# Powers on GpSimd in place of square roots and their corrections, in an eigensolver that runs under a graph network's products

## The chip, the cores and the metric

One core of a Trainium2 chip runs the program. The time is that of the device, in microseconds, as the median of three executions; a separate profiled execution gives the trace. Everything is computed in fp32. The engines are named as in the profile: PE (TensorE), with PEld for its weight loads, DVE (VectorE), ACT (ScalarE), POOL (GpSimd) and SP (the queue that issues the DMAs).

## What is computed

Two residual layers on `x` of 64 batches, 256 nodes and 256 features, with an adjacency matrix of 256 x 256. Layer 0 is three graph convolutions with the element-wise square of the adjacency; layer 1 needs the eigenvectors of a normalized Laplacian and applies a small network between `U.T` and `U`.

```python
def _L0_gnn_ref(x, adj, S, W1, W2, W3):          # S is adj
    def _slconv(x, adj, S, W):
        support = jnp.einsum('bnf,fh->bnh', x, W)
        return jnp.einsum('nm,bmh->bnh', adj * S, support)
    h = jax.nn.relu(_slconv(x, adj, S, W1))      # 256 -> 512
    h = jax.nn.relu(_slconv(h, adj, S, W2))      # 512 -> 1024
    return _slconv(h, adj, S, W3)                # 1024 -> 256

def _L1_gnn_ref(features, A, W1, b1, W2, b2):
    deg = jnp.sum(A, axis=0) + jnp.sum(A, axis=1) - jnp.diagonal(A)
    d_inv_sqrt = jnp.where(deg > 0, jax.lax.rsqrt(deg), 0.0)
    L_norm = d_inv_sqrt[:, None] * (jnp.diag(deg) - A) * d_inv_sqrt[None, :]
    _, U = jnp.linalg.eigh(L_norm)
    h = jax.nn.relu(jnp.einsum('mn,bnd->bmd', U.T, features) @ W1 + b1)
    return jnp.einsum('nm,bmd->bnd', U, h @ W2 + b2)

h = jnp.maximum(_layernorm(x, axis=-1), 0.0)
x = x + _L0_gnn_ref(h, adj, adj, W1, W2, W3)
h = jnp.maximum(_layernorm(x, axis=-1), 0.0)
x = x + _L1_gnn_ref(h, adj, W1, b1, W2, b2)
```

## The kernel before

**Two kinds of work share the core.** The eigensolver (class `Eigen`) is a long chain of small dependent instructions, mostly on DVE, with a few products on PE and a few copies and square roots on ACT. Layer 0 (class `Layers`) is a large amount of dense products on PE, whose results ACT copies or rectifies out of PSUM. Layer 1 can begin only when the eigenvectors are there. The 64 batches are worked on as 32 pairs; layer 0's results of most pairs are written to DRAM and fetched again for layer 1.

**The planner sets the order on PE and ACT.** Every instruction passes as an `Op` (line 83) through a `Pace` (line 161). `Op` gives each a planned duration by engine and size; for POOL it is `0.2 + 2 * n / 960` us for n elements in a partition. `Pace` keeps a planned clock for each engine. `chain` (line 211) takes an instruction of the eigensolver: it works out when its operands would be ready, and `run` (line 227) first issues as many instructions of the two layer-0 streams as fit ahead of that moment, cutting a product's columns in two where that fits better. `issue` (line 209 calls the instruction) multiplies the planned durations of the chain by `slower`: 1.06 as a rule (`SLOWER`), 1.13 in the leaves (`IN_BLOCKS`). The order made so is final for PE and ACT, which work through their queues in order. On DVE, POOL and SP the tile framework orders the instructions itself by its own estimates. Since nearly all instructions pass through `issue`, most rows of the profile carry L209; those after the planner is switched off carry L213.

**The stages of the chain**, in order:

- `laplacian` (line 402): degrees, their inverse square root `dinv` (by `root`, line 349: a square root on ACT, then a reciprocal, two sums or products and a scaling on DVE, then one more reciprocal), the matrix `A`.
- `tridiagonalize` (line 439): 254 Householder steps, `k` from 0. While `lo = k + 1` is under 128, a step works on both halves of the rows (the wide half), then on the second alone (the narrow half). `below` takes the sum of squares below the diagonal (`tail`), `length` the squared length `nn`, its root `s0` on ACT, half the sign `q` and `qn = q * nn`; the step then takes `rs = 1 / s0`, `qs = q * s0`, and `nb = rs * qn + qs`. In the trace nb is written to `m`. In the wide half `q`, `qn`, `qs`, `gg`, `gu` and part of `xc` run on POOL (`aside`), in the narrow half on DVE. `none` and a copy of `alpha` run on POOL in both. Two groups of transposes on PE bring the columns `ac` (as `psB<-ident,ac`) and `A`'s column (as `psA<-ident,A`) into rows; four long updates write the two halves of `A` at the end of a step, of which some stand behind the next step's `nn` on DVE.
- `reflections` (line 583), a third stream, forms the product of the reflections during the first part of `leaves` (line 983), which solves the 16 x 16 blocks on DVE with small roots on ACT and one copy on POOL in each iteration.
- `level` (line 1304), four times, for blocks of 32, 64, 128 and 256: it merges pairs of blocks. Its products are, in order, `psC<-ident,dnew`, `psC<-m,dnew`, `psA<-A,m`, `psA<-q,m`, `psB<-ident,m` and `psA<-q,m`. Between the first `psA<-q,m` and `psB<-ident,m` lies `rational_steps` (line 1213): a start and five iterations, each with one root of a [128, 2] column `dq` (in the trace `rdq`) on ACT. Then come `zh` and `rn`, each a `root` and a reciprocal. Ahead of the first `psA<-q,m` stands a root of a 256-wide row (`sq`).
- `vectors` (line 1718) ends the chain with a flag (`psC<-bad`), and the program branches on it; the branch that would solve again is not taken.

**The norms of layer 0.** `norm` (line 1835) serves both layer norms, once for each pair: ACT sums the four rows of a pair into `s`, DVE makes the negated mean `nm`, ACT sums the squares into `v`, DVE scales `v`, ACT takes the root, and five DVE instructions correct it and form `scale` and `shift`, which ACT needs for the normalized ReLU `h`.

**The end.** `layer1` (line 2131) runs layer 1's 32 pairs in a pipeline of three stages. What is left of layer 0 is put between its products; ahead of its ninth round, `pace.finish()` issues all that is still left. The pairs 30 and 31 stay on chip and come as the twelfth and thirteenth.

Of the kernel before, what the change touches and what calls it, by code (L numbers as in the profile page):

```python
# [82 lines left out]
class Op:  # L83
# [4 lines left out]
    def __init__(self, part, call, args, kwargs):  # L88
# [14 lines left out]
        if self.engine == "PE":  # L103
            self.columns = 0 if "transpose" in self.name else n
            self.busy = max(n * self.COLUMN, 0.224) if self.columns else 0.115
            self.until = max(self.busy, 0.165) + 0.35
        elif self.engine == "ACT":
            pointers = any(isinstance(kwargs.get(k), bass.AP) for k in ("scale", "bias"))
            self.busy = 0.13 + n / 1400 + 0.12 * pointers + 0.19 * sums
            self.until = self.busy + 0.12  # L110
        elif self.engine == "DVE":
            each = 6.3 if self.name == "reciprocal" else 2.0 if self.name == "tensor_tensor_scan" else 1.0
            pointers = self.name == "scalar_tensor_tensor" or any(a.shape[1:] == [1] for a in ins[1:])
            self.busy = 0.065 + 0.06 * pointers + each * n / 960 + 0.08 * sums
            self.until = self.busy + 0.125
        elif self.engine == "POOL":
            self.busy = 0.2 + 2 * n / 960
            self.until = self.busy + 0.1
        else:
            self.busy, self.until = 0.1, 4.0  # L120
# [40 lines left out]
class Pace:  # L161
# [5 lines left out]
    WINDOW = 1.0  # L167
    SLOWER, IN_BLOCKS = 1.06, 1.13
    LATER = {"PE": 0.4, "ACT": 0.1}
# [111 lines left out]
class Eigen:  # L281


    def __init__(self, tc, ctx, ap, gt2, pace):
# [11 lines left out]
        self.iota, self.far, self.ones = (pool.tile([P, N], F32, name=c) for c in ("iota", "far", "ones"))  # L296
        tc.nc.vector.memset(self.ones, 1.0)

        self.nc.scalar.activation(self.far[:, 0:1], self.ones[:, 0:1], AF.Sqrt)
# [46 lines left out]
    def recip(self, out, a):  # L346
        return self.nc.vector.reciprocal(out, a)

    def root(self, out, a, tmp, scale=1.0):
# [52 lines left out]
    def laplacian(self):  # L402
# [13 lines left out]

        safe, rt, tmp = self.col("c3"), self.col("c4"), self.col("c5")
        self.ts(safe, deg, 1e-30, OP.max)
        self.root(rt, safe, tmp)
        dinv = self.col("c6")  # L420
        self.recip(dinv, rt)
        self.stt(dinv, deg, 0.0, dinv, OP.is_gt, OP.mult)
# [16 lines left out]
    def tridiagonalize(self, a):  # L439
# [43 lines left out]
        def length(xr, lo, tail):  # L483

            nn, s0, q, qn = (self.col(c, 1) for c in ("nn", "s0", "q", "qn"))
            x1 = xr[:, lo : lo + 1]
            self.stt(nn, x1, x1, tail, OP.mult, OP.add)
            nc.scalar.activation(s0, nn, AF.Sqrt, bias=guard)
            aside(lo).tensor_scalar(q, x1, 0.0, 0.5, OP.is_ge, OP.subtract)
            aside(lo).tensor_tensor(qn, q, nn, OP.mult)  # L490
            return nn, s0, q, qn
# [7 lines left out]
        for k in range(N - 2):  # L499
# [5 lines left out]

            rs, qs, nb = self.col("rs", 1), self.col("qs", 1), nbs[:, k : k + 1]
# [24 lines left out]
            gc, gr = self.col("gc"), row("gr")  # L531
            self.ts(gc[:, hs], ac[:, hs], gam, OP.mult)

# [679 lines left out]
    def rational_steps(self, n, kd, zsum, zown, znxt, acc, s, gap, half, y, bs, rb):  # L1213
# [33 lines left out]
        for step in range(ROOT_STEPS):  # L1247
# [40 lines left out]
            self.ts(dq, dq, 1e-36, OP.max)  # L1288
            nc.scalar.activation(dq, dq, AF.Sqrt)
            self.tt(b, b, dq, OP.add)  # L1290
# [13 lines left out]
    def level(self, n, qt, dc, rho, sg, bad=None):  # L1304
# [452 lines left out]
class Layers:  # L1757


    def __init__(self, tc, ctx, ap, gt2, u, ut):  # L1760
# [22 lines left out]
        self.u1 = pool.tile([P, H], F32, name="u1")  # L1783
        self.ub2 = pool.tile([P, H, N], F32, name="ub2")

    def load_weights(self):
# [48 lines left out]
    def norm(self, x, scale, shift, parts=range(4)):  # L1835
# [3 lines left out]
        at = slice(parts[0], parts[-1] + 1, parts[1] - parts[0])  # L1839
        s, nm, v, tmp = (self.sp.tile([P, g], F32, tag=c, name=c) for c in ("s", "nm", "v", "tmp"))  # L1840
        for j in parts:
            junk = self.sp.tile([P, N], F32, tag="junk", name="junk", bufs=1)
            yield nc.scalar.activation(junk, x[:, j // 2, j % 2, :], AF.Copy, accum_out=s[:, j : j + 1])
        yield nc.vector.tensor_scalar(nm[:, at], s[:, at], -1.0 / N, None, OP.mult)
        for j in parts:
            junk = self.sp.tile([P, N], F32, tag="junk", name="junk", bufs=1)
            yield nc.scalar.activation(
                junk, x[:, j // 2, j % 2, :], AF.Square, bias=nm[:, j : j + 1], accum_out=v[:, j : j + 1]
            )
        s, nm, v, tmp, scale, shift = (t[:, at] for t in (s, nm, v, tmp, scale, shift))  # L1850
# [371 lines left out]
```

## Time and profile before

| | |
|---|---|
| median of 3 executions | 2425.47 us (2423.66 to 2426.67) |
| the profiled execution's own time | 2425.03 us |
| its span, first to last instruction | 2423.2 us |
| PE busy | 2380.5 us, 98% of the span, 9222 records |
| DVE busy | 2074.8 us, 86%, 12688 |
| ACT busy | 1014.1 us, 42%, 2827 |
| POOL busy | 479.1 us, 20%, 1752 |
| DMA | 90 MB, 37 GB/s on average; 250 GB/s from 2300 us on |
| chain of waits that ended last | PE from 2183 us to the end, but for 5.2 us at 2279 to 2285 |

Busy time is what an engine's records cover; a matmul's end is modelled, so that a PE that is busy all the time may still have small pauses between the starts of its products. The profile puts idle time of an engine down to what ended it (`<-` and an engine with a tile). Buffer numbers are left out of the names, and some short names stand for several tiles (`m`, `q`, `s`).

### The profile page before, as it was taken

How to read it: one execution, taken by the hardware profiler on the slowest of the kernel's cores; microseconds unless marked ns; L12 is line 12 of the kernel's file. 1: busy time of each engine (PE TensorE's matmuls, PEld its weight loads, DVE VectorE, ACT ScalarE, POOL GpSimd, SP SyncE). 2: the span in 40 equal slices, each digit the busy share in tenths (PEclk: the TensorE clock that was granted, in tenths of full speed). 3: DMA queues.
4: the chain of work that ended last, by engine and by line, in shares of the span. 5: the costliest groups of instructions: out<-in, count | busy, mean ns of one | idle time of the engine just before them, and what ended most of it. 6: DMA issues, size and time to landing. Idle time of an engine off the chain costs nothing. (4 is left out here: it accounts for less than half of the span.)

```text
span 2423.2 us, 38086 instructions
## 1 busy us (share of the span) xinstructions
PE 2380.5 (98%) x9222; PEld 1581.2 (65%) x9222; DVE 2074.8 (86%) x12688; ACT 1014.1 (42%) x2827; POOL 479.1 (20%) x1752
## 2 busy tenths in 40 slices
PE   7999999999999999999999899999999999999999
PEld 4666666666666566666666666666666666666887
DVE  7999999999999999999999999999878888861243
ACT  4444454444444443344444244444444343443322
POOL 2334333333333111111111000000000000002243
PEclk9999999999999999999999999999999999999999
DMA  3000000000000000000000000000000000002375
GB/s 114 18 17 11 23 23 18 23 23 19 10 23 19 22 22 23 22 6 23 23 23 26 10 23 22 23 23 22 18 27 22 22 23 5 22 23 107 114 253 196
DMA packets 59398, 90.02 MB, mean 37 GB/s; under 512 B 5792, under 2 KB 42784, under 8 KB 59168
## 3 DMA queue, kind: packets, MB, share of 16 engines
q1 hardware_dynamic: 59168, 87.52, 10.8%
q8 instruction: 75, 1.23, 0.2%
q14 instruction: 155, 1.27, 0.2%
HBM read 47.13 MB, written 40.37 MB: 36 GB/s over the span
## 5 line engine op out<-in xcount | busy, mean ns | idle before, releaser
L209 PE MATMUL bank<-y,L_gnn_W 128*128 128x512 f32 (+2 forms) x2180 | 906.7, 567 | 1.1 <-ACT y L209 1.1
L209 PEld LDWEIGHTS bank<-y,L_gnn_W 128*128 128x128 f32 x2180 | 401.4, 190 | 430.8 <-issue 408.5
L209 PE MATMUL bank<-L_gnn_W,s 128*128 128x256 f32 (+1 forms) x2092 | 468.0, 376 | 2.8 <-ACT s L209 2.8
L209 PEld LDWEIGHTS bank<-L_gnn_W,s 128*128 128x128 f32 x2092 | 388.4, 191 | 52.3 <-ACT s L209 3.3
L209 ACT ACTIVATE s<-bank 128x512 f32<-128x512 f32 x384 | 225.1, 586 | 217.6 <-PE bank L209 214.4
L209 PE MATMUL bank<-gt,s 128*128 128x256 f32 x1036 | 233.4, 377 | 0.4 <-ACT s L209 0.4
L209 PE MATMUL bank<-L_gnn_W,y 128*128 128x512 f32 (+2 forms) x538 | 230.9, 572 | 1.3 <-ACT y L209 1.1
L209 PEld LDWEIGHTS bank<-gt,s 128*128 128x128 f32 x1036 | 193.2, 190 | 36.2 <-issue 10.5
L209 ACT COPY y<-bank 128x512 f32<-128x512 f32 x192 | 111.2, 580 | 132.6 <-PE bank L209 132.2
L209 PEld LDWEIGHTS bank<-L_gnn_W,y 128*128 128x128 f32 x538 | 99.5, 190 | 98.0 <-issue 92.1
L209 ACT ACTIVATE s<-nn,guard 128x1 f32<-128x1 f32 x254 | 74.5, 293 | 207.9 <-DVE nn L209 169.3
L209 POOL COPY m<-xr 128x1 f32<-128x1 f32 x254 | 55.5, 218 | 535.2 <-DVE xr L209 523.2
L209 ACT ACTIVATE h<-x,shift,scale 128x256 f32<-128x256 f32 x256 | 137.7, 589 | 51.1 <-DVE shift L209 51.0
L209 ACT ACTIVATE junk<-x,nm 128x256 f32<-128x256 f32 x256 | 129.0, 504 | 31.6 <-DVE nm L209 27.1
L209 ACT ACTIVATE junk<-x 128x256 f32<-128x256 f32 x256 | 105.6, 412 | 85.5 <-DVE x L209 73.6
L209 DVE SCALAR_TENSOR_TENSOR A<-xr,wc,A 128x255 f32<-128x255 f32 (+63 forms) x381 | 139.7, 368 | 0.0
L209 DVE SCALAR_TENSOR_TENSOR A<-wr,q,A 128x255 f32<-128x255 f32 (+63 forms) x381 | 138.9, 366 | 0.0
L209 ACT ACTIVATE junk<-xr 128x254 f32<-128x254 f32 (+63 forms) x127 | 46.0, 362 | 216.3 <-DVE xr L209 211.3
L209 POOL TENSOR_TENSOR xb<-x,ub 128x512 f32<-128x512 f32 x16 | 19.8, 1267 | 552.9 <-ACT s L209 489.1
L209 PE MATMUL bank<-gt,h 128*128 128x256 f32 (+1 forms) x520 | 122.1, 384 | 0.1
L209 PE MATMUL bank<-p,gt 128*128 128x512 f32 (+2 forms) x270 | 117.8, 570 | 0.0
L209 DVE SCALAR_TENSOR_TENSOR r<-A,xr 128x255 f32<-128x255 f32 (+63 forms) x381 | 115.9, 304 | 0.1
(626 smaller groups left out, 4266.5 us busy)
## 6 DMA issues: line engine op xcount, KB each, us to landing
x<-x SPq DMA_DIRECT2D x60, 512.0 KB, 3.4
x<-in_x_dram SPq DMA_DIRECT2D x64, 256.0 KB, 3.7
out_dram<-out SPq DMA_DIRECT2D x64, 256.0 KB, 2.2
hw<-hw SPq DMA_DIRECT2D x60, 256.0 KB, 2.7
L_gnn_W<-in_L_gnn_W_dram SPq DMA_DIRECT2D x1, 2048.0 KB, 11.4
L_gnn_W<-in_L_gnn_W_dram SPq DMA_DIRECT2D x1, 1024.0 KB, 13.9
L_gnn_W<-in_L_gnn_W_dram SPq DMA_DIRECT2D x1, 512.0 KB, 6.8
mask<-in_c_blk_dram SPq DMA_DIRECT2D x2, 256.0 KB, 2.7
```

Source lines behind the costliest of these rows:

```text
L209: return op.call(*op.args, **op.kwargs)
```

## The change

The power instruction of GpSimd (`tensor_tensor` with `OP.pow` and a constant tile of exponents) takes the place of roots and of the instructions around them:

- in the Laplacian, one power of -0.5 for `dinv`;
- in the wide half, one power of 0.5 for `s0`; `q` stays on POOL, and `nb = 2 * q * s0` replaces `qn`, `rs`, `qs` and the old sum. The narrow half keeps its way, with the same instructions on DVE as before;
- in `rational_steps`, a power for the root of `dq`, 24 in all;
- in `level`, a power of -0.5 for `zh` and for `rn`;
- in `norm`, ACT's first pass is scaled so that it gives `nm` at once; `v`, the power of -0.5 that gives `scale`, and `shift` run on POOL.

Beside that, `u1` in both halves and `gc` in the narrow half are computed as a sum or product of two columns, not with a scalar read through a pointer. The planner charges a power `0.2 + 0.14 * n + 0.15` us, and multiplies the chain's durations by 0.97 in the levels (`IN_LEVELS`), by 1.06 again after them.

```diff
@@ Op
         elif self.engine == "POOL":
-            self.busy = 0.2 + 2 * n / 960
+            power = OP.pow in args
+            self.busy = 0.2 + (0.14 * n + 0.15 if power else 2 * n / 960)
@@ Pace
-    SLOWER, IN_BLOCKS = 1.06, 1.13
+    SLOWER, IN_BLOCKS, IN_LEVELS = 1.06, 1.13, 0.97
@@ Eigen
+        self.powers = {0.5: pool.tile([P, H], F32, name="half"), -0.5: pool.tile([P, H], F32, name="less")}
+        for y, t in self.powers.items():
+            tc.nc.vector.memset(t, y)
...
+    def power(self, out, a, y):
+
+        return self.nc.gpsimd.tensor_tensor(out, a, self.powers[y][:, 0 : out.shape[-1]], OP.pow)
@@ laplacian
-        self.root(rt, safe, tmp)
-        dinv = self.col("c6")
-        self.recip(dinv, rt)
+        self.power(dinv, safe, -0.5)
@@ tridiagonalize, length
+            if lo < P:
+                self.power(s0, nn, 0.5)
+                nc.gpsimd.tensor_scalar(q, x1, 0.0, 0.5, OP.is_ge, OP.subtract)
+                return nn, s0, q, None
             nc.scalar.activation(s0, nn, AF.Sqrt, bias=guard)
-            aside(lo).tensor_scalar(q, x1, 0.0, 0.5, OP.is_ge, OP.subtract)
-            aside(lo).tensor_tensor(qn, q, nn, OP.mult)
+            self.ts(q, x1, 0.0, OP.is_ge, 0.5, OP.subtract)
+            self.tt(qn, q, nn, OP.mult)
             return nn, s0, q, qn
@@ tridiagonalize, step
-            self.recip(rs, s0)
-            aside(lo).tensor_tensor(qs, q, s0, OP.mult)
+            if qn is not None:
+                rs, qs = self.col("rs", 1), self.col("qs", 1)
+                self.recip(rs, s0)
+                self.tt(qs, q, s0, OP.mult)
...
-                if h == halves[0]:
+                if h == halves[0] and qn is not None:
                     self.stt(nb, rs, qn, qs, OP.mult, OP.add)
+            if qn is None:
+                self.stt(nb, q, 2.0, s0, OP.mult, OP.mult)
...
-            self.ts(u1, u1, nb, OP.add)
+            self.tt(u1, u1, nb, OP.add)
...
-            self.ts(gc[:, hs], ac[:, hs], gam, OP.mult)
+            if halves[0]:
+                self.tt(gc[:, hs], ac[:, hs], gam, OP.mult)
+            else:
+                self.ts(gc, ac, gam, OP.mult)
@@ rational_steps, twice
-        nc.scalar.activation(dq, dq, AF.Sqrt)
+        self.power(dq, dq, 0.5)
@@ level
-        self.recip(zp, zp)
-        self.root(zh, zp, tmp)
+        self.power(zh, zp, -0.5)
...
-        self.root(rn, nrm, tmp)
-        self.recip(rn, rn)
+        self.power(rn, nrm, -0.5)
@@ join
-        self.pace.slower, self.pace.lead = self.pace.SLOWER, 0.0
+        self.pace.slower, self.pace.lead = self.pace.IN_LEVELS, 0.0
         for n in LEVELS:
             dc = self.level(n, zt, dc, self.rho, self.sg, bad)
+        self.pace.slower = self.pace.SLOWER
@@ norm
         for j in parts:
             junk = self.sp.tile([P, N], F32, tag="junk", name="junk", bufs=1)
-            yield nc.scalar.activation(junk, x[:, j // 2, j % 2, :], AF.Copy, accum_out=s[:, j : j + 1])
-        yield nc.vector.tensor_scalar(nm[:, at], s[:, at], -1.0 / N, None, OP.mult)
+            yield nc.scalar.activation(
+                junk, x[:, j // 2, j % 2, :], AF.Copy, scale=-1.0 / N, accum_out=nm[:, j : j + 1]
+            )
...
-        yield nc.vector.tensor_scalar(v, v, 0.25 / N, 0.25 * LN_EPS, OP.mult, OP.add)
-        yield nc.scalar.activation(s, v, AF.Sqrt)
-        yield nc.vector.reciprocal(tmp, s)
-        yield nc.vector.tensor_tensor(tmp, tmp, v, OP.mult)
-        yield nc.vector.tensor_tensor(s, s, tmp, OP.add)
-        yield nc.vector.reciprocal(scale, s)
-        yield nc.vector.tensor_tensor(shift, nm, scale, OP.mult)
+        yield nc.gpsimd.tensor_scalar(v, v, 1.0 / N, LN_EPS, OP.mult, OP.add)
+        yield nc.gpsimd.tensor_tensor(scale, v, self.rsqrt[:, 0 : scale.shape[-1]], OP.pow)
+        yield nc.gpsimd.tensor_tensor(shift, nm, scale, OP.mult)
```

More of the change, by code (lines that the diff above doesn't have):

```diff
@@ L415, in laplacian @@
         self.tt(deg, deg, dg, OP.subtract)
-        safe, rt, tmp = self.col("c3"), self.col("c4"), self.col("c5")
+        safe, dinv = self.col("c3"), self.col("c6")
         self.ts(safe, deg, 1e-30, OP.max)
-        self.root(rt, safe, tmp)
-        dinv = self.col("c6")
-        self.recip(dinv, rt)
+        self.power(dinv, safe, -0.5)
         self.stt(dinv, deg, 0.0, dinv, OP.is_gt, OP.mult)
@@ L504, in tridiagonalize @@
             rc = a[:, :, lo]
-            rs, qs, nb = self.col("rs", 1), self.col("qs", 1), nbs[:, k : k + 1]
-            self.recip(rs, s0)
-            aside(lo).tensor_tensor(qs, q, s0, OP.mult)
+            nb = nbs[:, k : k + 1]
+            if qn is not None:
+                rs, qs = self.col("rs", 1), self.col("qs", 1)
+                self.recip(rs, s0)
+                self.tt(qs, q, s0, OP.mult)
             xa, junk = self.col("xa"), self.row("r0")
@@ L1288, in rational_steps @@
             self.ts(dq, dq, 1e-36, OP.max)
-            nc.scalar.activation(dq, dq, AF.Sqrt)
+            self.power(dq, dq, 0.5)
             self.tt(b, b, dq, OP.add)
@@ L1784, in __init__ @@
         self.ub2 = pool.tile([P, H, N], F32, name="ub2")
+        self.rsqrt = pool.tile([P, 2 * H], F32, name="rsqrt")
+        self.nc.vector.memset(self.rsqrt, -0.5)
     def load_weights(self):
@@ L1839, in norm @@
         at = slice(parts[0], parts[-1] + 1, parts[1] - parts[0])
-        s, nm, v, tmp = (self.sp.tile([P, g], F32, tag=c, name=c) for c in ("s", "nm", "v", "tmp"))
-        for j in parts:
-            junk = self.sp.tile([P, N], F32, tag="junk", name="junk", bufs=1)
-            yield nc.scalar.activation(junk, x[:, j // 2, j % 2, :], AF.Copy, accum_out=s[:, j : j + 1])
-        yield nc.vector.tensor_scalar(nm[:, at], s[:, at], -1.0 / N, None, OP.mult)
+        nm, v = (self.sp.tile([P, g], F32, tag=c, name=c) for c in ("nm", "v"))
         for j in parts:
@@ L1847, in norm @@
             yield nc.scalar.activation(
-                junk, x[:, j // 2, j % 2, :], AF.Square, bias=nm[:, j : j + 1], accum_out=v[:, j : j + 1]
+                junk, x[:, j // 2, j % 2, :], AF.Copy, scale=-1.0 / N, accum_out=nm[:, j : j + 1]
             )
-        s, nm, v, tmp, scale, shift = (t[:, at] for t in (s, nm, v, tmp, scale, shift))
-        yield nc.vector.tensor_scalar(v, v, 0.25 / N, 0.25 * LN_EPS, OP.mult, OP.add)
-        yield nc.scalar.activation(s, v, AF.Sqrt)
-        yield nc.vector.reciprocal(tmp, s)
-        yield nc.vector.tensor_tensor(tmp, tmp, v, OP.mult)
-        yield nc.vector.tensor_tensor(s, s, tmp, OP.add)
-        yield nc.vector.reciprocal(scale, s)
-        yield nc.vector.tensor_tensor(shift, nm, scale, OP.mult)
+        for j in parts:
+            junk = self.sp.tile([P, N], F32, tag="junk", name="junk", bufs=1)
+            yield nc.scalar.activation(
+                junk,
+                x[:, j // 2, j % 2, :],
+                AF.Square,
+                bias=nm[:, j : j + 1],
+                accum_out=v[:, j : j + 1],
+            )
+        nm, v, scale, shift = (t[:, at] for t in (nm, v, scale, shift))
+        yield nc.gpsimd.tensor_scalar(v, v, 1.0 / N, LN_EPS, OP.mult, OP.add)
+        yield nc.gpsimd.tensor_tensor(scale, v, self.rsqrt[:, 0 : scale.shape[-1]], OP.pow)
+        yield nc.gpsimd.tensor_tensor(shift, nm, scale, OP.mult)
     def relu_norm(self, x, scale, shift, h, parts=range(4)):
```

## The prediction

> **What bounds the kernel now.** I read the granted clock first (0.998 on the one core: nothing is throttled for long), then busy time by stage, with the stages cut where the timeline shows the first and last `psB<-ident,ac` of the tridiagonalization, `psD<-mask,bs` (end of the reflections), `psB<-ident,m` (end of the leaves) and `psC<-bad` (end of the levels).
>
> ```profile
> core 0: us, PE busy (x) PEld busy (x) DVE busy (x) ACT busy (x) POOL busy (x), PEclk, DMA share, GB/s
> 0.00:22.60 22.60, 10.40 (x26) 6.24 (x27) 11.97 (x74) 11.03 (x32) 1.80 (x10) 1.00 0.91 286
> 22.60:770.00 747.40, 740.47 (x2937) 482.89 (x2938) 716.08 (x3697) 350.53 (x1062) 291.67 (x1134) 1.00 0.06 19
> 770.00:1322.70 552.70, 549.37 (x2144) 356.36 (x2144) 532.68 (x4196) 238.30 (x647) 98.75 (x511) 1.00 0.06 20
> 1322.70:1376.40 53.70, 47.22 (x241) 37.24 (x240) 48.60 (x309) 12.02 (x28) 0.46 (x2) 0.97 0.05 15
> 1376.40:1702.50 326.10, 322.06 (x1118) 203.40 (x1117) 305.37 (x2483) 133.75 (x384) 6.75 (x31) 0.99 0.07 22
> 1702.50:2178.00 475.50, 473.38 (x1739) 304.90 (x1738) 386.56 (x1816) 202.64 (x544) 0.00 (x0) 1.00 0.06 21
> 2178.00:2423.20 245.20, 237.63 (x1025) 190.13 (x1023) 73.52 (x119) 65.87 (x132) 79.70 (x64) 0.99 0.49 166
> ```
>
> TensorE is busy in every stage, and VectorE nearly so until 2178 us. A busy PE hides small stalls, so I counted its work. In the timeline consecutive matmul records start 429, 322, 216 and 109 ns apart for 512, 384, 256 and 128 columns; an fp32 product is two records, a transpose one. The program has 1322, 50, 2255 and 452 products of these widths and 1062 transposes outside the branch that isn't taken: 1135 + 32 + 973 + 99 + 116 = **2355 us of PE work** in a span of 2423.2. The other 68.3 us are PE stalls. Start of a product less the work issued ahead of it gives their place: 16.4 us before the first panel step, 13.8 in the wide half (k up to 126), 8.3 in the narrow half, 9.9 in the reflections, 6.7 in the leaves, 3.8 in the levels, 3.4 after them, 5.95 behind the last product. The eigen chain is no bound by itself: layer 0 left over at its end is done later at the same PE rate. **Only PE stalls can be won or lost.** A stall comes where the planner put less layer-0 work ahead of a chain product than the chain takes.
>
> **What the change does to the PE.** The compiled order has the same sum of 2355.0 us, placed otherwise: wide 733.5 to 715.5 us, narrow 544.5 to 542.8, reflections 43.7 to 50.1, leaves 319.4 to 314.6, levels 471.8 to 433.1, after them 235.9 to 293.2. So stage by stage: does the chain shrink as much as its filling?
>
> **Wide half.** One step's middle, VectorE and GpSimd:
>
> ```profile
> 405.20 0.24 POOL L209 TENSOR_SCALAR none<-m 128x1 f32<-128x1 f32 x1
> 405.52 0.21 POOL L209 TENSOR_TENSOR qn<-q,nn 128x1 f32<-128x1 f32 x1
> 405.69 0.38 POOL L209 TENSOR_TENSOR none<-none,nn 128x1 f32<-128x1 f32 x1
> 406.03 0.39 POOL L209 TENSOR_TENSOR qs<-q,s 128x1 f32<-128x1 f32 x1
> ...
> 405.61 0.16 DVE L209 RECIPROCAL rs<-s 128x1 f32<-128x1 f32 x1
> 405.68 0.35 DVE L209 SCALAR_TENSOR_TENSOR r<-A,xr 128x194 f32<-128x194 f32 x1
> ...
> 406.45 0.22 DVE L209 SCALAR_TENSOR_TENSOR m<-rs,qn,qs 128x1 f32<-128x1 f32 x1
> ```
>
> The instruction `m<-` (nb) waits for qs: 107 of 126 steps, 9.7 us. The changed step drops qn, qs, the ScalarE root and the reciprocal, and puts one power on POOL where qn stands. Savings on VectorE, by the distance to the next start (durations overlap): the reciprocal 73 ns x 126 = 9.5; the wait for qs 9.7; u1 as a sum of two columns 47 ns x 126 = 6 (124 ns with the pointer scalar, 77 for `gg<-z`); the seven small norm instructions, 147 here, 14.1 busy and 4.6 of waits = 18.7. Sum 44. The PE waits of 6.0 (`r<-psB,xr`) go with them: 747 - 50 = 697 us of chain against 715.5 of filling. The chain then waits for PE, not PE for it; I leave 2.5 us for uneven steps. **-11 us.**
>
> This rests on the power. From qn's start to the moment at which nb could start without the reciprocal are 0.9 us early in this half and 0.68 in its last quarter. The trace has no power; bounds: 0.2 us (the shortest POOL instruction of one column, 0.19) and 1.3 (its longest tensor_tensor, 1.27 for 512 columns). I take 0.5, by the nearest row: qs, 0.38, and 0.1 on top. Then nb doesn't wait, and `none`, queued behind the power on POOL, ends before den needs it. gg and gu also stand behind the norms' three POOL instructions (0.2 + 0.8 + 0.2 us, 21 times here); c needs gg 2 us after nb, so they just fit.
>
> **A rule that speaks against it.** The Trainium skill, "SBUF — State Buffer", section "Who interferes with whom": a VectorE instruction with two SBUF inputs and a GpSimd instruction that reads SBUF exclude each other, and the later one blocks till the other is done. The trace shows it once, behind a long POOL instruction:
>
> ```profile
> 2278.33 2.50 POOL L213 TENSOR_TENSOR xb<-x,ub 128x512 f32<-128x512 f32 x2 [5.26 <-issue]
> ...
> 2279.84 1.01 DVE L209 TENSOR_TENSOR tmp<-tmp,v 128x4 f32<-128x4 f32 x1
> ```
>
> tmp takes 1.01 us instead of 0.16 and ends with xb. But in the step above the updates of A take 0.42 us with a short POOL instruction beside them and without one; there only POOL waits. By the rule a power blocks an update for up to 0.5 us: 126 x 0.5 = 63 us, 760 us of chain, 44 of stalls. By the rows of one column it blocks nothing[...]. I follow these rows and keep the rule as rival B.
>
> **Narrow half.** u1 and gc as sums of columns, 2 x 47 ns x 127 = 12; norms 9.5 + 2.9; PE waits 2.6. 553 - 27 = 526 against 542.8 (the planner charges the new forms as it did the old): stalls 8.3 to 1.5, **-7 us.**
>
> **Reflections, leaves, start.** Reflections keep their chain, with 6.4 us more PE work in it; two stalls of about 2.8 us each cost 1.7 more by a lower clock (granted 0.72 over 1344 to 1350). 9.9 to 6: **-4.** Leaves: chain shorter by the norms' 7 us, filling by 4.8; the large stall there comes from a ReLU waiting for shift, now on POOL: **0**, give or take 4. Start: the Laplacian's root, 1.7 us on ScalarE and VectorE, becomes one power behind two norm instructions on POOL: **0**, give or take 1.5.
>
> **Levels.** What VectorE waits for there:
>
> ```profile
> DVE rb L209 <- ACT rdq L209: 30.8, 21, 5.3
> DVE tmp L209 <- ACT rn L209: 9.7, 4, 4.1
> DVE v L209 <- ACT junk L209: 3.8, 2, 2.4
> DVE tmp L209 <- ACT zh L209: 1.4, 4, 0.5
> ```
>
> The 24 roots of rdq take ScalarE 0.2 us, but stand behind its evacuations and ReLUs (5.3 us at worst). On an idle POOL: 0.6 and two hops of 0.1, 24 x 0.8 = 19 for 30.8: -12. zh and rn lose ten dependent VectorE instructions of 0.2 us in each level: -4. Norms: 9.7 busy and 8.1 of waits: -18. Together -34. Now the chain's products start 0.1 to 0.9 us after their operand is ready, some 15 us in all, so the chain alone took 460 and takes 426, for 433 of filling. But 0.97 for 1.06 shortens all of it alike, also the part from `psA<-A,m` to `psA<-q,m`, whose root stays: 3.2, 2.6, 3.9, 4.7 us less filling in the four levels, where 0.6 to 0.9 of margin and a norm's 1.2 stand against it. That leaves stalls of 0.5 to 3 us in each: 3.8 to 7, **+3.**
>
> **After the levels.** 57 us more of layer 0 is left. In the kernel before, the last pair's norm was covered by layer 1:
>
> ```profile
> 2272.13 1.02 PE L209 MATMUL bank<-p,gt 128*128 128x512 f32 x2
> 2272.99 1.03 PE L209 MATMUL bank<-hw,u 128*128 128x256 f32 x4
> ...
> 2280.76 1.89 PE L209 MATMUL bank<-L_gnn_W,g 128*128 128x256 f32 x8
> 2282.48 0.27 PE L209 MATMUL bank<-eye,h 128*128 128x128 f32 x1
> 2283.60 1.26 PE L209 MATMUL bank<-eye,h 128*128 128x128 f32 x7 [0.85 <-ACT h L209]
> ```
>
> Nine us of layer 1 stand between the last `p,gt` and `eye,h`. In the new order everything left is issued before layer 1's ninth pair, and the eight `eye,h` follow `p,gt` at once. Exposed: add 0.9, two sums at 0.54, four squares at 0.63, POOL 1.5 with hops, four ReLUs at 0.5, transposes and their copy 1.4 = 9.4, less 0.9 of work; 0.7 for p's copy; 1.7 for the clock, as after the stalls above. About 11 for 2 before: **+9.5 us.**
>
> **Sum.** -11 - 7 - 4 + 0 + 3 + 9.5 = -9.5: a span of 2413.7. The profiled execution took 2425.03 with a span of 2423.2; the median, 2425.47, lies 2.3 above that span: **2416 us.**
>
> **Rivals.** A change under 0.2% (4.9 us) can't be told from none.
> - **A, as summed: 0.60**, own range 2406 to 2424; nearly all of it faster.
> - **B, the power holds VectorE up, by its length or by the shared port: 0.22.** For: no row for a power, and the row of tmp. Against: the short POOL rows. A's wide half takes 715.5 + 2.5 = 718. A step held up for 0.35 us (a power less the 0.15 in which VectorE still ends an instruction) gives 697 + 44 = 741, 23 above that: 2439. From 0.24 us a step on (697 + 30 = 727, where A's 9.5 are used up) it is slower than before.
> - **C, stalls won in the panel are given back in levels and tail: 0.18.** For: the filling shrinks by 8% in the levels, uncovered roots of 256 columns remain. Against: the removed queue behind ScalarE. Another 2.5 us in each level: 2426.
>
> The range takes A whole and B's nearer part: 2406 to 2436. Faster: 0.55 of A and 0.04 of C; same 0.05, 0.12 and 0.02 of B; slower 0.02 of C and 0.20 of B: 0.59, 0.19, 0.22.
>
> **What would show it.** Wide half: its last product some 30 us earlier, nb without a wait for POOL, updates of A still near 0.42 us at this width, PE waits at psB nearly gone. Levels: no wait of rb for ScalarE, end near 2100 us. Tail: one PE stall of 7 us or more at `eye,h`, and a granted clock under 1 behind it. A power above 1 us, or updates stretched by the power, would make me wrong.

## The result: slower, where faster was forecast

The changed kernel takes **2438.95 us** (2437.80 to 2439.58), the kernel before 2425.47, five executions of each: a ratio of 1.0055, with a 95% interval of 1.004 to 1.007. The profiled execution has a span of 2437.2 us where it had 2423.2. The forecast was 2416, with a range up to 2436.

The PE work is 2355.0 us as before, so again only stalls of PE count. The first view of the profile after is the busy time of each stage, cut at the same products as before (each row: stage, its length, then busy time and instructions of PE, its weight loads, VectorE, ScalarE and GpSimd, the granted clock, the DMA share and GB/s):

```profile
core 0: us, PE busy (x) PEld busy (x) DVE busy (x) ACT busy (x) POOL busy (x), PEclk, DMA share, GB/s
0.00:21.30 21.30, 9.52 (x25) 5.66 (x26) 9.53 (x58) 10.94 (x29) 4.94 (x16) 1.00 0.91 296
21.30:757.10 735.80, 726.48 (x2907) 478.33 (x2908) 688.51 (x3458) 309.18 (x890) 331.65 (x1076) 1.00 0.06 19
757.10:1303.20 546.10, 544.95 (x2149) 357.71 (x2148) 516.53 (x4077) 233.01 (x627) 119.33 (x551) 1.00 0.06 21
1303.20:1357.00 53.80, 47.89 (x222) 32.97 (x222) 49.87 (x329) 20.07 (x53) 3.43 (x7) 1.00 0.04 12
1357.00:1675.30 318.30, 315.66 (x1075) 195.28 (x1074) 296.52 (x2364) 129.31 (x367) 21.39 (x61) 1.00 0.07 22
1675.30:2127.30 452.00, 439.31 (x1620) 284.80 (x1621) 369.78 (x1677) 177.24 (x448) 42.85 (x69) 0.99 0.06 19
2127.30:2437.20 309.90, 297.51 (x1225) 228.33 (x1224) 71.82 (x107) 90.73 (x190) 85.25 (x76) 0.98 0.40 135
```

The chain does get shorter: it ends at 2127.3 us, where it ended at 2178.0. But what follows it takes 309.9 us, where it took 245.2. Work was moved to the end and stalls were added on the way. The same count of stalls as in the prediction (start of a product less the work issued ahead of it), for every kernel of this study:

| stalls, us | start | wide | narrow | reflections | leaves | levels | after them | behind last product | sum | median, us | ratio to before (95%) |
|---|---|---|---|---|---|---|---|---|---|---|---|
| before | 16.4 | 13.8 | 8.3 | 9.9 | 6.7 | 3.8 | 3.3 | 6.0 | 68.2 | 2425.5 | |
| forecast for the change | 16.4 | 2.5 | 1.5 | 6 | 6.7 | 7 | 12.9 | 6.0 | 59 | 2416 | |
| **after** | 15.4 | 15.1 | 4.5 | 7.8 | 3.7 | 18.9 | 12.6 | 4.1 | 82.2 | 2439.0 | 1.0055 (1.004 to 1.007) |
| e1_norms_back | 14.0 | 8.7 | 4.0 | 11.8 | 3.6 | 21.2 | 13.3 | 4.1 | 80.6 | 2438.3 | 1.0059 (1.0042 to 1.0076) |
| e2_clock_back | 16.6 | 14.9 | 4.4 | 7.8 | 3.5 | 4.2 | 14.0 | 4.1 | 69.5 | 2426.1 | 1.0009 (1.0000 to 1.0017) |
| e4_last_at18 | 14.1 | 14.8 | 4.4 | 7.8 | 3.4 | 18.8 | 2.7 | 4.1 | 70.2 | 2428.5 | 1.0018 (1.0011 to 1.0025) |
| e6_level_roots_back | 15.0 | 14.9 | 4.4 | 7.8 | 3.6 | 10.7 | 13.4 | 5.7 | 75.6 | 2432.3 | 1.0032 (1.0019 to 1.0044) |
| k2_zh_back | 15.9 | 14.7 | 4.5 | 7.8 | 3.5 | 17.2 | 13.7 | 4.1 | 81.4 | 2438.0 | 1.0058 (1.0042 to 1.0073) |
| f1_clock_last18 | 14.5 | 14.9 | 4.5 | 7.9 | 3.6 | 4.2 | 3.2 | 4.2 | 57.0 | 2414.6 | 0.9962 (0.9949 to 0.9976) |
| f3_f1_pool_ordered | 13.0 | 24.9 | 11.3 | 7.8 | 3.9 | 11.3 | 3.3 | 4.2 | 79.8 | 2438.7 | 1.0060 (1.0047 to 1.0074) |
| e5_norms_clock_back | 13.8 | 9.0 | 4.1 | 11.8 | 3.9 | 16.4 | 2.0 | 4.1 | 64.9 | 2423.2 | 0.9995 (0.9987 to 1.0003) |
| h4_wide_norms_vector | 13.8 | 9.0 | 4.6 | 8.7 | 7.1 | 7.9 | 2.0 | 4.1 | 57.1 | 2413.5 | 0.9956 (0.9942 to 0.9970) |
| g1_wide_power_only | 15.2 | 10.7 | 7.1 | 8.9 | 3.9 | 4.2 | 3.4 | 4.1 | 57.4 | 2415.6 | 0.9966 (0.9954 to 0.9978) |
| g3_sums_only | 15.4 | 12.9 | 4.3 | 9.9 | 6.8 | 3.8 | 3.3 | 4.1 | 60.6 | 2418.1 | 0.9977 (0.9968 to 0.9987) |
| h2_norms_only | 15.3 | 15.9 | 9.1 | 9.2 | 5.7 | 2.5 | 13.3 | 6.2 | 77.2 | 2433.8 | 1.0037 (1.0024 to 1.0051) |
| h1_before_097 | 13.9 | 13.9 | 8.4 | 8.3 | 6.9 | 12.1 | 12.1 | 4.1 | 79.5 | 2440.4 | 1.0068 (1.0053 to 1.0083) |
| k1_power_and_sums | 14.1 | 9.6 | 3.7 | 10.6 | 3.9 | 4.2 | 3.4 | 4.1 | 53.4 | 2411.9 | 0.9951 (0.9938 to 0.9965) |

The stalls of each row are those of one profiled execution; that of h1 took 2436.35 us and was the fastest of its four, 4.1 us under the median. Kernels with the same order up to the panel differ by 2 us at the start (after, e2, e4), so single differences of that size there are not read. In the ratios each kernel is compared with the kernel before of its own round, whose median lay between 2423.9 and 2425.5 us, so that a difference of 1 or 2 us between medians of different rounds says nothing. Below, a kernel is called by the first two characters of its name.

Three places of the trace of after carry the loss. **The wide half.** The waits of VectorE from 21.3 to 757.1 us, and the same two in the kernel before, from 22.6 to 770.0 us (us in total, times, longest):

```profile
DVE m L210 <- POOL s L210: 14.1, 30, 1.6
DVE r L210 <- PE psB L210: 13.2, 36, 1.3
...
DVE r L209 <- PE psB L209: 5.3, 16, 0.4
DVE m L209 <- POOL qs L209: 1.1, 3, 0.7
```

The power `s` makes VectorE wait 30 times, 14.1 us in all, at most 1.6; qs did so three times. (The view counts waits from 0.15 us on.) One such step, GpSimd's and VectorE's timelines (start, duration, then what it waited for in brackets):

```profile
536.50 0.36 POOL L210 TENSOR_SCALAR v<-v 128x4 f32<-128x4 f32 x1 [2.21 <-ACT junk L210]
536.95 1.23 POOL L210 TENSOR_TENSOR scale<-v,rsqrt 128x4 f32<-128x4 f32 x1
538.13 0.18 POOL L210 COPY m<-xr 128x1 f32<-128x1 f32 x1
...
539.23 0.56 POOL L210 TENSOR_TENSOR s<-nn,half 128x1 f32<-128x1 f32 x1
...
536.78 0.22 DVE L210 SCALAR_TENSOR_TENSOR nn<-xr,m 128x1 f32<-128x1 f32 x1
...
539.82 0.16 DVE L210 SCALAR_TENSOR_TENSOR m<-q,s 128x1 f32<-128x1 f32 x1 [1.65 <-POOL s L210]
```

The operand `nn` is there at 537.0. The power starts at 539.2, because the norm's `v` stood at the head of GpSimd's queue for 2.2 us, waiting for ScalarE's squares, and the norm's own power of four columns took 1.2 more. The step's copy, sign and power came behind them. PE then stalls 1.3 us at `psB<-ident,ac`. Stalls at this product, in 22 of 126 steps, are 10.9 of the wide half's 15.1 us. Seven of them, 6.6 us together, follow a norm on GpSimd, and in each of the seven nb waits 0.8 to 1.6 us for its power. The largest of the others, 1.5 us, comes in a step in which nb does not wait at all.

**The levels.** The place with the longest stall, in the level of 64; GpSimd, VectorE and PE:

```profile
1874.32 0.19 POOL L210 TENSOR_SCALAR v<-v 128x4 f32<-128x4 f32 x1 [7.57 <-ACT junk L210]
1874.60 1.01 POOL L210 TENSOR_TENSOR scale<-v,rsqrt 128x4 f32<-128x4 f32 x1
1875.69 0.20 POOL L210 TENSOR_TENSOR shift<-nm,scale 128x4 f32<-128x4 f32 x1
1875.84 0.70 POOL L210 TENSOR_TENSOR zh<-zp,less 128x2 f32<-128x2 f32 x1
...
1870.91 0.17 DVE L210 TENSOR_SCALAR zp<-zp 128x2 f32<-128x2 f32 x1
1876.57 0.16 DVE L210 TENSOR_TENSOR zh<-zh,tmp 128x2 f32<-128x2 f32 x1 [5.49 <-POOL zh L210]
...
1866.64 7.25 PE L210 MATMUL bank<-y,L_gnn_W 128*128 128x512 f32 x18
1877.89 1.22 PE L210 MATMUL psA<-q,m 128*128 128x128 f32 x4 [3.99 <-DVE m L210]
```

`zp` is ready at 1871.1 and its power starts at 1875.8: 4.8 us behind a norm. PE stands still for 4.0 us, and the clock that it is granted afterwards is half (stretch, length, PE busy, clock):

```profile
1878.00:1881.00 3.00, 3.00 (x7) 0.50 0.00 0
1881.00:1884.00 3.00, 3.00 (x7) 0.56 0.01 3
1884.00:1888.00 4.00, 4.00 (x12) 1.00 0.00 0
```

That is 2.9 us more. These 7.1 us, and stalls of 0.5 to 3.0 us ahead of some other products of the levels, make up the 18.9. The waits of PE from 1676.0 to 2127.3 us (2.2 us in all in the levels of the kernel before):

```profile
PE psA L210 <- DVE m L210: 4.0, 1, 4.0
PE bank L210 <- DVE x L210: 3.2, 2, 1.6
PE psC L210 <- DVE m L210: 2.8, 4, 1.8
PE psB L210 <- DVE m L210: 2.0, 2, 1.1
PE psA L210 <- ACT u L210: 0.7, 1, 0.7
```

The first is the stall behind `zh`. The second is layer 0's own: two of its products wait for a sum `x` that stands on VectorE behind the chain's work in rational_steps. psC stands at the start of a level (`psC<-m,dnew`), psB the product behind rational_steps.

**The end.** PE's timeline where layer 0 runs out:

```profile
2286.06 3.68 PE L210 MATMUL bank<-p,gt 128*128 128x512 f32 x8
2296.48 0.48 PE L210 MATMUL bank<-eye,h 128*128 128x128 f32 x1 [6.74 <-ACT h L210]
2297.47 1.82 PE L210 MATMUL bank<-eye,h 128*128 128x128 f32 x7 [0.51 <-ACT h L210]
```

No layer-1 product stands between the last `p,gt` and `eye,h`, and the last pair's norm is bare.

### The profile page after: what moved, and what is told of

Its sections match the earlier page's. It is cut to its first block, busy times and chain, and to the rows that moved or that the text cites. A ratio compares the mean times of both kernels' runs of the same rounds, so it can differ in the third digit from the quotient of the medians.

```text
span 2437.2 us, 37126 instructions
## 1 busy us (share of the span) xinstructions
PE 2381.3 (98%) x9216; PEld 1583.1 (65%) x9216; DVE 2002.5 (82%) x12064; ACT 970.5 (40%) x2602; POOL 608.8 (25%) x1853
## 3 DMA queue, kind: packets, MB, share of 16 engines
q1 hardware_dynamic: 59168, 87.52, 10.7%
## 5 line engine op out<-in xcount | busy, mean ns | idle before, releaser
L210 PE MATMUL bank<-y,L_gnn_W 128*128 128x512 f32 (+3 forms) x2176 | 911.6, 569 | 3.2 <-DVE x L210 3.2
L210 PE MATMUL bank<-gt,s 128*128 128x256 f32 (+1 forms) x1036 | 234.0, 377 | 1.4 <-ACT s L210 0.7
L210 PEld LDWEIGHTS bank<-gt,s 128*128 128x128 f32 x1036 | 192.9, 190 | 39.5 <-issue 12.6
L210 ACT ACTIVATE s<-nn,guard 128x1 f32<-128x1 f32 x127 | 37.3, 293 | 194.8 <-DVE nn L210 171.9
L210 DVE SCALAR_TENSOR_TENSOR chain<-coef,chain 128x2 f32<-128x2 f32 x448 | 96.9, 216 | 9.1
## 6 DMA issues: line engine op xcount, KB each, us to landing
L_gnn_W<-in_L_gnn_W_dram SPq DMA_DIRECT2D x1, 2048.0 KB, 11.1
```

Of the source, the lines that this page charges most:

```text
L210: return op.call(*op.args, **op.kwargs)
```

## The experiments

Two theories at first. **Filling:** 0.97 leaves too little layer-0 work in the levels, and too much behind them. **Queue:** the norm's first GpSimd instruction waits for ScalarE at the head of GpSimd's queue, with the chain's powers behind it. In each text, stalls are those of the table.

### The clock of the levels, alone

`e2_clock_back`, on the changed kernel:

```diff
-    SLOWER, IN_BLOCKS, IN_LEVELS = 1.06, 1.13, 0.97
+    SLOWER, IN_BLOCKS, IN_LEVELS = 1.06, 1.13, 1.06
```

> The changed kernel with 1.06 on the planner's clock in the levels in place of 0.97. The filling of the levels is 472.6 us of PE work in place of 433.1, and 253.7 us are left after them in place of 293.2; no layer-1 work stands between the last pair's layer-0 product and its transposes, as in the changed kernel. Filling theory: the chain of the levels now waits for PE and not PE for it; stalls there fall from 18.9 to 5 or less, those after the levels stay near 12; 2425. Queue theory: the long stall in the level of 64 stays nearly whole (some 3 us, and the low clock behind it), stalls in the levels near 11; 2431.

2426.13 us: of 13.5 us of loss 2.0 are left with this one number, and the stalls in the levels are 4.2. Filling holds. The queue theory had the long stall of the level of 64 stay; it went: with other filling the norms came elsewhere in the order, and `zh` found GpSimd free.

`h1_before_097` makes the opposite edit, on the kernel before:

```diff
-        self.pace.slower, self.pace.lead = self.pace.SLOWER, 0.0
+        self.pace.slower, self.pace.lead = 0.97, 0.0
         for n in LEVELS:
             dc = self.level(n, zt, dc, self.rho, self.sg, bad)
+        self.pace.slower = self.pace.SLOWER
```

> The kernel before with 0.97 in the levels alone (1.06 again after them); no power anywhere. Filling of the levels 427.4 us in place of 471.8; nothing stands between the last pair's layer-0 product and its transposes, in place of 9.5 us. Filling theory: the chain of the levels takes some 455 us by itself, so stalls there become about 30, and those after them about 12: 2424 + 26 + 9 = 2459. Queue theory (the loss in the levels needs norms and powers together on POOL): stalls in the levels near 10, 2440.

2440.41 us, by 8.3 us more stalls in the levels and 8.8 after them. So 0.97 alone, without any power, makes as slow a kernel as the whole change. But 30 us of stalls did not come: there are 12.1 in the levels. That is near the 10 of the queue theory, though its reason can't be the cause in a kernel without any power. The waits of VectorE in these levels show why:

```profile
DVE rb L209 <- ACT rdq L209: 11.1, 22, 2.7
DVE tmp L209 <- ACT rn L209: 8.3, 4, 3.9
```

rb waited 30.8 us for ScalarE in the kernel before. With 44 us less layer-0 work in the same stretch it waits 11.1, and the old chain ends its levels in 439.5 us (1698.7 to 2138.2), not in the 460 that the prediction took for it. Some 20 of the 30.8 us went with the filling, of which ScalarE has its share.

### The end, alone

`e4_last_at18`:

```diff
-LAST_AT = 12
+LAST_AT = 18
```

> The changed kernel with the last layer-0 work issued ahead of layer 1's fifteenth round in place of its ninth, and the two pairs that stay on chip put in places 18 and 19. The order is the same up to the end of the chain. 14.7 us of layer-1 products then stand between the last pair's layer-0 product and its transposes, in place of none. If the tail's loss is the uncovered norm of the last pair: the stall of 6.9 us at the transposes and the slower clock behind it go, stalls after the levels fall from 12.6 to about 4; 2430. If the end is bound by its transfers: the gain is given back, 2437 to 2439.

2428.54 us, and 2.7 us of stalls after the levels in place of 12.6. The bare norm is the tail's loss.

### Both together

`f1_clock_last18` has both edits.

> The changed kernel with both edits that each gave time back: 1.06 in the levels, and the last layer-0 work ahead of layer 1's fifteenth round. If the two losses are separate (stalls in the levels from 18.9 to 4.2, stalls after them from 12.6 to 2.7), they add up: 2416, faster than the kernel before by 8 us. If the work that the first moves ahead of the end takes from the second: 2424.

2414.63 us. The two losses are separate and add up; with them undone, the rest of the change is worth 10 us.

### The norms

`e1_norms_back` puts the norm back as it was before:

```diff
-        yield nc.gpsimd.tensor_scalar(v, v, 1.0 / N, LN_EPS, OP.mult, OP.add)
-        yield nc.gpsimd.tensor_tensor(scale, v, self.rsqrt[:, 0 : scale.shape[-1]], OP.pow)
-        yield nc.gpsimd.tensor_tensor(shift, nm, scale, OP.mult)
+        yield nc.vector.tensor_scalar(v, v, 0.25 / N, 0.25 * LN_EPS, OP.mult, OP.add)
+        yield nc.scalar.activation(s, v, AF.Sqrt)
...
```

> The changed kernel with the norms done as before (sums on ScalarE, scaling and correction on VectorE, root on ScalarE), everything else as changed. Queue theory (the norm's first POOL instruction waits for ScalarE at the head of POOL's queue, and the chain's copies and powers stand behind it): VectorE's waits for the power s (13.5 us, 29 times in the wide half) fall under 4 us, the wait of zh for its power in the level of 64 (5.5 us) goes, and with it the low clock behind it; PE stalls in the levels fall from 18.9 to about 10. VectorE pays the norms' small instructions again. Sum about 2426. Filling theory (0.97 leaves too little layer-0 work in the levels, whoever does the norms): the levels, filled by 437.3 us of PE work in place of 433.1, keep stalls of 17 or more; 2437.

2438.29 us. In the wide half the queue theory is right: stalls 15.1 to 8.7. In the levels it falls: 21.2. There VectorE's own queue now has the norm's instruction at its head (in the level of 128 `v` waits 2.91 us for ScalarE, ahead of the chain's reciprocal), PE stalls 4.3 us at `psA<-q,m`, and the clock takes 2.7 more.

`e5_norms_clock_back` has 1.06 as well.

> The changed kernel with the norms as before and 1.06 in the levels; powers in the chain and sums of columns stay. The filling of the levels is 477.8 us, and 12.1 us of layer-1 products stand between the last pair's layer-0 product and its transposes. With the norms off POOL the first half of the stalls is 21.7 us to step 120 (29.7 with the norms there), those of the levels about 4 as in clock_back, those after them about 3 as in the kernel before: 2412. If the norms are no matter but for their place in the order: 2418 to 2420.

2423.18 us, a miss by 11: the wide half and the tail came as expected, but the levels kept 16.4 us of stalls (VectorE's `v` and `nm` wait 11.1 us for ScalarE there, a product `psA<-q,m` stalls 3.4 us, and in the last two levels PE itself waits 1.8 and 2.2 us for ScalarE to bring a layer-0 result out of PSUM).

`h2_norms_only` is the kernel before with the norm as changed, and nothing else.

> The kernel before with the norms on POOL alone; roots and sums as before, 1.06 in the levels. POOL carries qn, qs, none, gg and gu of the wide half, and the norms' instructions stand among them. If it is the norms that hold up the wide half on POOL: VectorE's waits for POOL there are over 8 us, and stalls up to step 120 grow from 29.2 to 33 or more. The filling of the levels is 466.0 us, stalls there stay near 4; nothing covers the last pair's norm, so 9 more after them: 2424 + 4 + 9 - 4 (narrow half, whose chain gets shorter) = 2433. If the queue is no matter: 2427.

2433.81 us. Nearly all of its loss is the tail's: the planner charges the new norm less, puts 21 us less filling ahead of the chain's end, and the last pair comes out bare. The queue shows in the wide half (6.2 us of waits for qs, the longest 1.5; stalls 13.8 to 15.9).

`h4_wide_norms_vector` is f1 with the old norm up to step 127 only:

```diff
+        if Pace.WIDE:
+            yield from self.norm_by_vector(x, scale, shift, parts)
+            return
```

> The kernel of clock_last18, with the norms done as before up to step 127 and on POOL from there on. Stalls up to step 120 should be near 22, as with all norms put back, in place of 28.5; from the narrow half on as in clock_last18 (5.4, 7.9, 3.6, 4.2, 3.2, 4.2): 2408. If the norms on POOL are worth as much in the wide half as they cost there: 2415.

2413.51 us. The wide half gives the 6 us (14.9 to 9.0), but leaves and levels take 7 of them back in the order that results (3.6 to 7.1, 4.2 to 7.9).

### The place in the queue

`f3_f1_pool_ordered` is f1 with GpSimd's instructions in the planner's order, those of PE and ACT unchanged:

```diff
-        with tc.manual_schedule(engines={mybir.EngineType.PE, mybir.EngineType.Activation}):
+        with tc.manual_schedule(engines={mybir.EngineType.PE, mybir.EngineType.Activation, mybir.EngineType.Pool}):
```

> The kernel of clock_last18 with POOL's instructions in the planner's order too, PE and ACT in the same order as there. In that order the norm's scale and shift no longer stand ahead of the next step's copy and power in some 10 of the norms of the wide half. If the queue on POOL is what the wide half's stalls are: 10.7 us of stalls between steps 20 and 120 become 6 or so, 4 us less than clock_last18. If not: within 2 us of it.

2438.70 us: 24 us slower than f1, by nothing but the order on GpSimd. The expectation had the sign wrong. In the panel, with 10.0 and 6.8 us more stalls in its halves, VectorE's den now waits 26.8 us for `none` on GpSimd, 2.0 in f1. In the levels, with 7.1 more, GpSimd's timeline shows how, here in the level of 64:

```profile
1873.17 0.19 POOL L210 TENSOR_SCALAR v<-v 128x4 f32<-128x4 f32 x1 [11.70 <-ACT junk L210]
...
1874.68 0.70 POOL L210 TENSOR_TENSOR rdq<-rdq,half 128x2 f32<-128x2 f32 x1
```

`v` holds the queue for 11.7 us, and the root of rational_steps comes behind it; VectorE waits 10.1 us for that one root.

`e6_level_roots_back` keeps norms and 0.97 and puts the levels' roots back on ScalarE:

```diff
-        self.power(dq, dq, 0.5)
+        nc.scalar.activation(dq, dq, AF.Sqrt)
...
-        self.power(zh, zp, -0.5)
+        self.recip(zp, zp)
+        self.root(zh, zp, tmp)
```

> The changed kernel with the levels' roots (rdq, zh, rn) done as before on ScalarE and VectorE; norms stay on POOL, 0.97 stays. The filling of the levels is 429.6 us in place of 433.1. Queue theory: zh no longer stands behind the norm (4.2 us of stall and 2.9 us of low clock in the level of 64 go), but the waits of rb for ScalarE come back (30.8 us before, 20.1 us for POOL now); stalls in the levels near 22, 2442. Filling theory: the chain is longer by 15 us with 3.5 us less filling, and all of it shows: stalls near 37, 2456.

2432.31 us, with 6.6 us fewer stalls than with the powers. The levels take 440.4 us in place of 452.0, with nearly the same filling. VectorE's rb waits 13.1 us for the 24 roots on ScalarE, where it waits 20.1 for the 24 powers, and zh 2.8 where it waits 7.9. So at 0.97 the powers there cost time; how much of it is the norms' other places in the order is not shown.

`k2_zh_back` moves `zh` alone:

```diff
-        self.power(zh, zp, -0.5)
+        self.recip(zp, zp)
+        self.root(zh, zp, tmp)
```

> The changed kernel with zh's root alone done as before; rdq, rn and the norms stay on POOL, 0.97 stays. The filling of the levels is 437.4 us in place of 433.1. If the stall of the level of 64 (4.2 us, and 2.9 us of low clock behind it) is that of zh queued behind the norm: both go, stalls in the levels fall from 18.9 to about 11; 2430. If the chain of that level is too long for its filling by itself: 15 or more, 2435 to 2438.

2437.98 us: the stall stays, and the theory that it is GpSimd's queue falls. VectorE in the level of 64:

```profile
1872.24 0.17 DVE L210 RECIPROCAL zp<-zp 128x2 f32<-128x2 f32 x1
1878.90 0.17 DVE L210 RECIPROCAL tmp<-zh 128x2 f32<-128x2 f32 x1 [6.49 <-ACT zh L210]
```

The order puts two whole norms, one behind the other, ahead of `zh`. On ScalarE `zh` stands behind their squares and ReLUs, on GpSimd behind the second one's `v`. For this stall the engine doesn't matter; being behind a norm does. In e6 the norms came elsewhere.

### The parts that are left, alone

`g1_wide_power_only` is the kernel before with the wide half's power:

```diff
+            if lo < P:
+                self.power(s0, nn, 0.5)
...
+            if qn is None:
+                self.stt(nb, q, 2.0, s0, OP.mult, OP.mult)
```

> The kernel before with one part of the change alone: the power in the wide half and nb = 2 q s0. If the power is short enough for its place and only the norms on POOL spoil it: stalls up to step 120 fall from 29.2 to about 22 (as with the norms put back), the rest as before: 2417. If a power of 0.72 us is too long for the step: no gain or a loss, 2424 to 2428.

2415.63 us, 8.6 less than the kernel before. VectorE's wait for the power in this kernel's wide half:

```profile
DVE m L210 <- POOL s L210: 4.0, 24, 0.2
```

Without a norm on GpSimd it waits 0.2 us at most, where it waited up to 1.6. But of the 10.8 us by which its stalls are fewer, only 3.1 lie in the wide half, where the power is; 2.8 lie in the leaves and 1.9 behind the last product, where this kernel has the instructions of the kernel before. Nothing here shows the power at work in these, and as far as the forecast goes they are luck.

`g3_sums_only`:

```diff
-            self.ts(u1, u1, nb, OP.add)
+            self.tt(u1, u1, nb, OP.add)
...
+            if halves[0]:
+                self.tt(gc[:, hs], ac[:, hs], gam, OP.mult)
```

> The kernel before with one part alone: u1 in both halves and gc in the narrow half as a sum or product of two columns. The order on PE is the same. If VectorE's 6 us in the wide and 12 us in the narrow half shorten the chain where PE waited for it: stalls fall by 2 in the wide and 4 in the narrow half, 2418. If the chain waits for PE there anyway: 2424.

2418.13 us, and the 4 us in the narrow half as expected (8.3 to 4.3).

`k1_power_and_sums` has both:

> The kernel before with the two parts that gave time alone: the power in the wide half (2415.6 alone) and the sums of columns (2418.1 alone); norms, levels and clocks as before. If the gains are those of separate stalls (8.6 and 6.1 us): they add up but for the 2 us by which the last output lands earlier in both, 2412. If both shorten the same stretch of VectorE and the rest of it was covered already: 2415.

**2411.88 us**, 0.49% faster than the kernel before (0.35 to 0.62) and the lowest median here, though the intervals of f1, g1 and h4 overlap with its own. The gains add up but for 2 us, as expected. What the change has beyond these two parts (norms on GpSimd, powers in the levels, 0.97) makes the loss. Most of it comes through 0.97 and the bare end: f1, which has neither but keeps norms and powers, is within 3 us of this kernel.

## Why the prediction was wrong, step by step

The stalls were to fall by 9.5 us and rose by 14.0. Of the 23 us between forecast and outcome, 12.6 lie in the wide half and 11.9 in the levels; the narrow half and the reflections gave 4.8 us less than forecast, and leaves, start, tail and the stretch behind the last product 6.2 more.

**The wide half (forecast -11, measured +1.3): the failed step is "Then nb doesn't wait", with "c needs gg 2 us after nb, so they just fit".** It set the norm's three GpSimd instructions, at their own 1.2 us, ahead of gg and gu alone. It left out that `v`, the first of them, waits for ScalarE, and that the chain's copy, sign and power stand behind it while it waits. The prediction looked at what stands behind the power, not at what the power stands behind. 14 such waits of `v` in the wide half are 18.6 us at the head of GpSimd's queue. This step is worth some 6.4 of the 12.6 us (15.1 to 8.7 with the norms off GpSimd, e1; 6.6 by the seven steps above). The other 6.2 are the "2.5 us for uneven steps", a term that was too small by itself: with the norms off GpSimd the wide half still stalls 8.7 to 10.7 us. Such stalls come in steps of their own, as that of 1.5 us above does; what makes each of them is open. The price of the power was too low as well (taken 0.5, measured 0.56 to 0.99, median 0.71). With the waits too short for the view, nb waited 9.7 us for qs in the kernel before, as the prediction counted, and waits 8.3 for the power in g1 and 21.1 in the changed kernel: that saving of 9.7 hardly came even without the norms.

**The rule of the shared port** was rightly not followed. In this trace 115 updates of A with at least half their time beside a power are 4 ns longer on average, 10 at most, than updates of the same width that run beside no power (most of them beside another GpSimd instruction). It is the power that gets longer beside VectorE's work (0.56 us in the step above, where VectorE idles). Rival B named 2439 us, which is what came out, but by a way that isn't in the trace.

**The narrow half (-7; -3.8).** The mechanism was right for the sums (g3: -4.0). The norms' part didn't come: in h2 the narrow half stalls 9.1 us, with some 3 us less filling than before. What else kept the chain from getting shorter is not shown.

**Leaves (0; -3.0) and start (0; -1.0)** are within what was allowed, **reflections (-4; -2.1)** gave half. Behind the last product 1.9 us went, though nothing was changed there. Most variants show 4.1, too; the kernel before, e6 and h2 show about 6. This stays open.

**The levels (+3; +15.1): the failed step is "the chain alone took 460 and takes 426, for 433 of filling".** Neither number holds. h1 shows the old chain done in 440 us once there is less filling, and after shows the new one at 452. The 12 us from "24 x 0.8 = 19 for 30.8" had the price of the power right (VectorE waits 20.1 us for the 24) and the gain wrong: the 30.8 shrank with the filling to 11.1 in h1 and 13.1 in e6, so that at 0.97 VectorE waits 7 to 9 us longer for the powers, where 12 were to be won. The 4 us for zh and rn didn't come either, since VectorE's waits for the two grew from 11.1 to 19.6 us, about as much as ten dropped instructions of 0.2 us save in four levels. And the 18 us of norms moved to another queue, where `zh` stands behind them. The prediction had looked for the stall between `psA<-A,m` and `psA<-q,m`, ahead of rational_steps; PE stalls 0.05 us at most ahead of those four products. The stalls came behind it: at `zh`, at `psB<-ident,m`, at the start of a level, and at layer-0 products that wait for VectorE. Of the 15, 0.97 alone makes 8.3 (h1), taking it back removes 14.7 (e2), and taking the powers out removes 8.2 (e6). The two overlap, so that the 15 can't be split between them. At 1.06 the powers in the levels bring nothing that shows: stalls of 4.2 with them (f1) and without (g1).

**The tail (+9.5; +9.3)** came as worked out, with the low clock behind it; e4 shows it from the other side.

**The rivals.** C, stalls won in the panel and given back in the levels and the tail, is the one that came (chance 0.18), and larger than its 2426 us: nearly 4 us more in each level where it had another 2.5 on top of the forecast's 0.8, and the wide half's gain, which C kept, was missing. What spoke against it, the removed queue behind ScalarE, was the filling's own.

## What to carry to other kernels

An instruction that waits for another engine costs its queue the wait, not its duration: before moving work onto a helper engine that the critical chain uses, ask which operand comes last and what stands behind it. A wait measured under filling is partly made by that filling, so it can't be counted as a gain when the filling is cut as well. And where PE's total work is fixed, a planner's clock that "fits" the chain is right only from one side: too much filling costs little here, too little costs stalls, a lower clock behind the long ones, and cover at the end.

## What had not been expected of the hardware

- Which gaps lower the clock. In the levels of all kernels here, PE gaps of up to 1.8 us (idle time in the profile's rows) left no trace in the next products. Of nine gaps of 2.0 to 3.2 us, seven cost 1.5 to 1.9 us each behind them, with a granted clock of 0.57 to 0.65 over the next 4 us (2.5 us in e6, 2.6 in h1); two cost nothing, with 1.00 (2.7 us in e1, 2.4 in f3). After the gap of 4.0 us in the changed kernel it was 0.50 to 0.56 for 6 us, and 2.9 us were lost; after 5.4 us in k2, 3.0. The Trainium skill, "TensorE: Matmul & The Clock Gate", Part 1, gives half rate after about 3.4 us of idleness, counted in a window that runs freely. The gaps of 4.0 us and more fit that, and a window that runs freely also fits that of nearly equal gaps some go free; that the clock falls behind 2.0 to 3.2 us of idleness at all is earlier than the page says.
- The power: 0.56 to 0.99 us for one column of 128 (0.56 with next to no VectorE work beside it, 0.73 on average where VectorE is busy all along), 0.70 for two columns, 1.04 on average for four. VectorE's updates of A beside it are 4 ns longer on average.
